# Sharing an activation-table stay between the Silu of z and the Silu of the next chunk's u

## The chip, the cores and the metric

The kernel runs on one core of a Trainium2 chip. The metric is the device time of one execution in microseconds (us), lower is better. A core has five engines that each work through their own instruction queue: TensorE (PE in the profile), VectorE (DVE), ScalarE (ACT), GpSimd (POOL) and SyncE (SP), which here only issues DMA transfers.

## The reference

The program is a stack of four residual layers on an image batch x of shape (8, 384, 32, 32), each `x = x + layer(groupnorm(x))`. Layers 0 and 2 are Mamba blocks, layer 2 with a layer norm before and an MLP behind; layers 1 and 3 are convolution blocks. The change touches only the Mamba blocks. Cut to what matters, one of them computes, for each image as a sequence of L = 1024 tokens:

```python
xz = x @ in_proj_w.T
xin, z = split(xz, 2)                  # 768 channels each
u = silu(causal_conv3(xin) + conv_b)
dt, Bm, Cm = split(u @ x_proj_w.T)     # 24, 16 and 16 columns
dt = softplus(dt @ dt_proj_w.T + dt_proj_b)
# for every channel d and state n (768 x 16):
h[t] = exp(dt[t] * A) * h[t-1] + dt[t] * u[t] * Bm[t]
y[t] = sum_n h[t] * Cm[t] + u[t] * D
y = y * silu(z)
return y @ out_proj_w.T
```

All inputs and outputs are fp32.

## The kernel before

**Tiling.** The work of a Mamba layer is cut into chunks of 512 tokens, two for each of 8 images and 16 for each of the two layers, so there are 32 chunks: 0 to 15 are layer 0, 16 to 31 are layer 2. The 768 channels are six blocks of 128, `NH` = 3 of them make a half. Each chunk has 24 steps (`NQ`); a step handles 32 channels times 16 states as four tiles of 128 x 512. The whole kernel is 768 steps in a fixed order, and everything else is threaded between them.

**One step.** A DMA broadcasts dt*u to a tile `g` of 128 x 2048 (`begins`, on SP, up to five such tiles). POOL multiplies `g` by B (`times`). PE spreads dt to the four PSUM tiles `dA` (`decays`), ACT turns each into exp(dt*A) in place (`exps`), DVE scans each tile (`scans`) and multiplies two of the four by C itself, POOL multiplies the other two by C (`states`), PE sums over the states into `y` (`gathers`). In the first chunk of an image ACT also copies the last column of each scan to `carry`, which the second chunk starts from. Every fourth step completes a channel block: DVE multiplies `y` by silu(z) (`gatings`), and this frees the single `y` bank for the next block.

**Table stays.** ACT holds one set of activation functions at a time. The steps need Exp and Ln; Silu and Gelu lie in other sets. So each visit to Silu or Gelu is a *stay*: a table load, the activations, and a load back, which `exp_set` (L369) issues at once. While it lasts the `exps` on ACT wait. There are four kinds: `gates(s, 0)` for the first half of z (z0 below), `gates(s, 1)` for the second half (z1), `front` for both halves of u, and the Gelus of layers 1 and 2. A stay starts only when `session` (L563) allows it: when at least `LEAD` = 2 exponentials are done that DVE has not scanned yet, or when it was held up for longer than `PATIENCE`.

**Who needs what.** z0 is used from the first gating of its chunk, z1 from the fourth, which follows step 15. The u of chunk n + 1 is projected while chunk n is in its steps 6 to 11, and its Silu must come early enough for x_proj, dt, softplus, three DMA stages (`dtd`, `dud` to DRAM and `dts`, `g` back) and POOL's first product before step 0 of chunk n + 1.

**Order.** Nothing is reordered on the chip: each engine's queue is written out in Python. `Order.run` (L219) holds generators such as `gates`, `front`, `finish`, `layer1`, and at each turn issues the next instruction of the one that the planner `Clocks` expects to begin first. Thus one instruction that begins at another planned time can shift which process comes next, on all engines. `once(test)` holds a process until a condition of the planner's state is true; `ahead["scans"]` counts scans issued, four for each step.

Of the kernel before, what the change touches and what calls it, by code (L numbers as in the profile page):

```python
# [11 lines left out]
AF = mybir.ActivationFunctionType  # L12
# [42 lines left out]
def _flat(ap):  # L55
    return ap.rearrange("p a b -> p (a b)")
# [193 lines left out]
def tile_conv_preact_d4(ctx: ExitStack, tc: tile.TileContext, a: dict, out: bass.AP):  # L250
# [23 lines left out]
    def new(pool, shape, dtype, tag, bufs=1, name=None):  # L274

        t = pool.tile(shape, dtype, tag=tag, name=name or tag, bufs=bufs)
        ring = rings.setdefault((id(pool), tag), [])
        if len(ring) >= bufs:
            clocks.born[t.name] = clocks.last.get(ring[-bufs], 0.0)
        ring.append(t.name)  # L280
        return t

    def on(engine, *aps, when=None, due=None, next_=False):


        def ready():
            t = when() if when else 0.0
            return None if t is None else max(t, clocks.known(*aps) if aps else 0.0)

        return engine, ready, due, next_  # L290
# [5 lines left out]
    def once(test):  # L296
        return None, lambda: 0.0 if test() else None, None, False

    class Tokens:
# [5 lines left out]
        def when(self):  # L305
            return min(self.free) if self.free else None
# [19 lines left out]
    def ps_give(ps, tag):  # L326
        banks.append((tag, clocks.last[ps.name]))
# [32 lines left out]
    def together(due, gens):  # L360

        made = [order.add(g, due) for g in gens]
        yield on(None, when=lambda: (
            None if any(p["done"] is None for p in made) else max(p["done"] for p in made)
        ))
# [3 lines left out]
    def exp_set():  # L369
        nc.scalar.preload_act_table_set(SET_EXP)  # L370
        clocks.free["ACT"] += 1.28
        act_set["now"] = "exp"

    def act(out_, in_, func, **kw):
        if func in (AF.Exp, AF.Ln):
            if act_set["now"] != "exp":
                exp_set()
        elif func not in (AF.Identity, AF.Copy, AF.Square, AF.Abs):
            if act_set["now"] != func:
                clocks.free["ACT"] += 1.28  # L380
            act_set["now"] = func
        scalar.activation(out_, in_, func, **kw)
# [175 lines left out]
    def projection(s, name, part, at):  # L558
        return chain(
            name, ((s["w"][part][:, k, at : at + P], s["xn"][:, k, :]) for k in range(KC))  # L560
        )

    def session():  # L563

        asked = []

        def ready():
            asked.append(order.now)
            late = order.now - asked[0] > PATIENCE
            late = late or ("begin", ahead["decays"] // 4) not in said  # L570
            return 0.0 if ahead["decays"] - ahead["scans"] >= LEAD or late or order.stuck else None

        return ready

    def gates(s, h):
        n = s["n"]
        yield once(lambda: "normed" in s and "loaded" in s["w"] and (n == 0 or chunks[n - 1]["gated"] >= (NH if h == 0 else ND)))
        z = s["z", h] = new(wk, [P, NH, T], F32, "z", 2)

        def block(d):  # L580
            ps, tag = yield from projection(s, "ps_z", "z", (h * NH + d) * P)
            yield on("ACT", ps)
            act(z[:, d, :], ps, AF.Copy)
            ps_give(ps, tag)

        yield from together(s["t"] + (6 if h else -4), [block(d) for d in range(NH)])
        yield on("ACT", z, when=session())
        act(_flat(z), _flat(z), AF.Silu)
        exp_set()
        s["gates", h] = True  # L590
# [30 lines left out]
    def front(s):  # L621
        c, n, due = s["c"], s["n"], s["t"] - 26
# [40 lines left out]
        if c > 0:  # L663
            yield on("POOL", *u, due=-1)
            prev = chunks[n - 1]["xt"]
            hal = new(wk, [P, ND, 3], F32, "hal")
            gpsimd.tensor_mul(
                hal[:, :, 0:2], prev, vec[:, :, 0:1].to_broadcast([P, ND, 2])
            )
            gpsimd.tensor_mul(hal[:, :, 2:3], prev[:, :, 1:2], vec[:, :, 1:2])  # L670
            gpsimd.tensor_add(hal[:, :, 0:1], hal[:, :, 0:1], hal[:, :, 2:3])
            for h in range(2):
                gpsimd.tensor_add(
                    uh[h][:, :, 0:2], uh[h][:, :, 0:2], hal[:, h * NH : (h + 1) * NH, 0:2]
                )
        yield on("ACT", *u, when=session())
        for h in range(2):
            act(_flat(uh[h]), _flat(uh[h]), AF.Silu)
        exp_set()
# [86 lines left out]
    ahead = {"decays": 0, "scans": 0}  # L766
# [499 lines left out]
    def layer3(s):  # L1266
# [68 lines left out]
    chunks = [  # L1335
        {"pre": pre, "src": src, "b": b, "c": c, "n": (q * B + b) * NCH + c, "gated": 0}
        for q, (pre, src) in enumerate((("l0_", a["x"]), ("l2_", x_mid)))
        for b in range(B)
        for c in range(NCH)
    ]  # L1340
# [4 lines left out]
    def start_jobs(t):  # L1345
        n, i = divmod(t, NQ)
        if i or n >= len(chunks):
            return
        s = chunks[n]
        order.add(gates(s, 1), t + 8)  # L1350
        if s["c"] == 0 and n + NCH < len(chunks):
            m = chunks[n + NCH]
            order.add(measured(m), t + NQ + 4)
        if n + 1 < len(chunks):
            later = chunks[n + 1]
            order.add(front(later), t + NQ - 26)
            order.add(gates(later, 0), t + NQ - 4)
        order.add(finish(s), t + NQ + 10)
# [15 lines left out]
    def begun():  # L1374
        yield once(lambda: "fronted" in chunks[0])
        order.add(gates(chunks[0], 0), 1)
        start_jobs(0)
# [3 lines left out]
    order.add(load_mamba("l0_"), 0)  # L1381
    order.add(load_mamba("l2_", chunks[B * NCH - 1]), NQ * B * NCH - 30)
    order.add(front(chunks[0]), 0)
    order.add(begun(), 0)
    order.add(diagonal(), 2)
# [151 lines left out]
```

## Time and profile before

| what | value |
|---|---|
| median of 3 runs | 6210.31 us (6209.75 to 6211.98) |
| the profiled execution: its own time, its span | 6204.07 us, 6202.2 us |
| DVE busy | 5616.8 us, 91% |
| POOL busy | 5725.3 us, 92% |
| PE busy | 5799.2 us, 94% |
| ACT busy | 4241.3 us, 68% |
| table loads | 288, of 1283 ns each, 369.6 us in all |
| Silu of half a z | 64, of 1485 ns each |
| Silu of half a u | 64, of 1477 ns each, two in each stay |

Busy is the time in which an engine executes something; the rest of the span is idle. 6202.2 us over 768 steps is 8.1 us for each step, start and end included; from the first step's scans to the last step's, the mean is 7.82 us. An instruction is named by the tile that it writes, an arrow, and the tiles that it reads: `dA<-dA,w_A` is one exponential. Nearly all instructions carry line 189, the line of a wrapper, so they are told apart by tiles and shapes; L370 is the load back of a stay.

### The profile page before, as it was taken

Reading aid. Unit: us, or ns where it says so; the run is one execution under the profiler, and the core shown is the slowest. Engines: PE = TensorE matmul, PEld = TensorE weight load, DVE = VectorE, ACT = ScalarE, POOL = GpSimd, SP = SyncE. Lnnn points to the kernel's source line nnn. Section 1 sums busy time; section 2 is a strip of 40 time slices with the busy share of each in tenths; the row PEclk is TensorE's granted clock in tenths of the full one; section 3 lists DMA queues with packets and bytes.
Section 4 is the critical chain, followed back from the end, with each engine's and each line's share of the span. In section 5 each row is a group of like instructions: output and inputs, shape, how many; then the busy total and the mean of one; then the engine's idle time right before and its main releaser. Section 6 shows DMA issues by size and latency. Waiting matters only on the chain.

```text
span 6202.2 us, 62614 instructions
## 1 busy us (share of the span) xinstructions
PE 5799.2 (94%) x19022; PEld 2184.1 (35%) x19022; DVE 5616.8 (91%) x6381; ACT 4241.3 (68%) x7942; POOL 5725.3 (92%) x2028
## 2 busy tenths in 40 slices
PE   6878999999999999999989999999999999999998
PEld 2223333333333333333333333333333333333333
DVE  5999999999998999998887899899998999989994
ACT  5656677677667767776676676777767777677753
POOL 4999999999999999989997999999999999999991
PEclk8889999999999999999999999999999999999999
DMA  6877878877887888787777888878888788888871
GB/s 178 193 184 186 195 190 194 204 188 193 190 193 185 196 205 189 192 205 186 180 185 183 199 196 219 200 198 209 198 215 201 200 207 198 212 205 197 207 197 58
DMA packets 346724, 1195.88 MB, mean 193 GB/s; under 512 B 40516, under 2 KB 142580, under 8 KB 248084
## 3 DMA queue, kind: packets, MB, share of 16 engines
q1 hardware_dynamic: 346388, 1191.88, 79.1%
q8 instruction: 152, 2.49, 0.2%
q14 instruction: 184, 1.51, 0.1%
HBM read 1040.73 MB, written 150.99 MB: 192 GB/s over the span
## 4 chain that ended last, share of the span: by engine, by line
DVE 25%; PE 13%; POOL 8%; DMA 4%; issue 4%; ACT 4%; SPq 0%; POOLq 0%; DVEq 0%; ACTq 0%
DVE g L189 11%; DVE dA L189 8%; POOL g L189 6%; DVE u L189 2%; PE ps_dn L189 2%; PE ps_up L189 2%; PE ps_dw L189 2%; PE y L189 2%; PE dA L189 2%; DMA g<-dud 2%; DVE ps_dw L189 1%; PE ps_z L189 1%; DMA dts<-dtd 1%; PE ps_out L189 1%; DVE st L189 1%
## 5 line engine op out<-in xcount | busy, mean ns | idle before, releaser
L189 POOL TENSOR_TENSOR g<-g,bc 128x1024 f32<-128x1024 f32 (+1 forms) x1536 | 5243.4, 3447 | 248.1 <-ACT carry L189 94.1
L189 ACT ACTIVATE dA<-dA,w_A 128x512 f32<-128x512 f32 x3072 | 2018.6, 661 | 931.0 <-PE dA L189 919.4
L189 PE MATMUL dA<-dts,selr 96*128 96x512 bf16 x3072 | 1190.0, 390 | 233.2 <-DVE g L189 207.6
L189 DVE TENSOR_TENSOR_SCAN g<-dA,carry,g 128x512 f32<-128x512 f32 x768 | 955.4, 1269 | 75.1 <-POOL g L189 61.1
L189 DVE TENSOR_TENSOR g<-dA,bc 128x512 f32<-128x512 f32 x1536 | 994.5, 677 | 17.3 <-ACT carry L189 16.4
L189 DVE TENSOR_TENSOR_SCAN g<-dA,g 128x512 f32<-128x512 f32 x768 | 909.4, 1209 | 85.7 <-POOL g L189 77.8
L189 DVE TENSOR_TENSOR_SCAN dA<-dA,carry,g 128x512 f32<-128x512 f32 x768 | 952.2, 1271 | 28.0 <-ACT dA L189 27.4
L189 DVE TENSOR_TENSOR_SCAN dA<-dA,g 128x512 f32<-128x512 f32 x768 | 909.0, 1212 | 62.3 <-ACT dA L189 61.7
L189 PE MATMUL y<-g,sely 128*32 128x512 f32 x6144 | 857.0, 627 | 38.0 <-POOL g L189 35.6
L189 PEld LDWEIGHTS <-selr 96*128 96x128 bf16 x3072 | 300.2, 98 | 1113.0 <-issue 1072.0
L189 PE MATMUL ps_in<-xf,w_in 128*128 128x512 f32 x1152 | 562.7, 610 | 10.0 <-ACT xf L189 7.6
L189 PE MATMUL ps_z<-xf,w_z 128*128 128x512 f32 x1152 | 567.8, 597 | 3.6 <-DVE dt L189 3.6
L189 PE MATMUL ps_up<-t,mw 128*128 128x512 f32 x1152 | 556.0, 596 | 7.1 <-DVE u L189 5.2
L189 PE MATMUL ps_out<-u,w_out 128*128 128x512 f32 x1152 | 547.5, 594 | 0.4 <-ACT carry L189 0.4
L189 PE MATMUL ps_dn<-h,mw 128*128 128x512 f32 x1152 | 545.3, 594 | 1.6 <-ACT h L189 1.6
L189 PE MATMUL ps_dw<-tp,diag 128*128 128x512 f32 x864 | 438.8, 609 | 9.6 <-ACT diag L189 9.6
L189 PEld LDWEIGHTS y<-g,sely 128*32 128x32 f32 x6144 | 126.3, 109 | 599.2 <-issue 313.0
L189 PEld LDWEIGHTS ps_in<-xf,w_in 128*128 128x128 f32 x1152 | 218.6, 195 | 263.8 <-issue 234.2
L189 POOL TENSOR_TENSOR dt<-dt,u 128x512 f32<-128x512 f32 x192 | 244.3, 1274 | 72.4 <-PE ps_dr L189 56.3
L189 PEld LDWEIGHTS ps_dn<-h,mw 128*128 128x128 f32 x1152 | 217.8, 190 | 259.9 <-issue 235.3
L189 PEld LDWEIGHTS ps_up<-t,mw 128*128 128x128 f32 x1152 | 214.4, 190 | 267.2 <-issue 230.4
L189 PEld LDWEIGHTS ps_z<-xf,w_z 128*128 128x128 f32 x1152 | 215.9, 191 | 252.7 <-issue 215.2
(118 smaller groups left out, 6451.1 us busy)
## 6 DMA issues: line engine op xcount, KB each, us to landing
g<-dud SPq DMA_DIRECT2D x768, 1024.0 KB, 8.2
dtd<-pc SPq DMA_DIRECT2D x192, 384.0 KB, 4.0
dts<-dtd SPq DMA_DIRECT2D x192, 384.0 KB, 7.8
mw<-in_l_mlp_w SPq DMA_DIRECT2D x192, 384.0 KB, 6.5
dud<-dt SPq DMA_DIRECT2D x768, 64.0 KB, 3.2
xf<-in_x SPq DMA_DIRECT2D x16, 768.0 KB, 9.1
x<-in_x SPq DMA_DIRECT2D x16, 768.0 KB, 11.9
x_mid<-x SPq DMA_DIRECT2D x16, 768.0 KB, 7.0
```

The costliest lines, as they stand in the source:

```text
L189: return call(out_, *args, **kw)
```

## The change

`gates(s, 1)` no longer goes into a stay of its own once z1 is projected. It leaves its tile in `s["gate"]` and waits. The `front` of the next chunk now waits until the previous chunk's `gate` entry exists, enters its stay, and there computes the Silu of that z1 ahead of the two of u. If `front` has not done so by the time 13 steps of the chunk are scanned in the planner's state, `gates` takes its tile back and goes into a stay of its own as before. The last chunk has no next one and stays as it was.

```diff
         yield from together(s["t"] + (6 if h else -4), [block(d) for d in range(NH)])
+        if h == 1 and n + 1 < len(chunks):
+            s["gate"] = z
+            yield once(lambda: ("gates", 1) in s or ahead["scans"] >= 4 * (s["t"] + 13))
+            if ("gates", 1) in s:
+                return
+            s["gate"] = None
         yield on("ACT", z, when=session())
         act(_flat(z), _flat(z), AF.Silu)
         exp_set()
...
+        prev = chunks[n - 1] if n > 0 else {"gate": None}
+        yield once(lambda: "gate" in prev)
         yield on("ACT", *u, when=session())
+        if prev["gate"] is not None:
+            act(_flat(prev["gate"]), _flat(prev["gate"]), AF.Silu)
+            prev["gates", 1] = True
         for h in range(2):
             act(_flat(uh[h]), _flat(uh[h]), AF.Silu)
         exp_set()
```

## The prediction

> **What bounds the kernel now.** I read the page's totals first, then the groups of instructions with shapes kept apart, then the waits, then windows over single stays.
>
> ```profile
> PE 5799.2 (94%) x19022; PEld 2184.1 (35%) x19022; DVE 5616.8 (91%) x6381; ACT 4241.3 (68%) x7942; POOL 5725.3 (92%) x2028
> ```
>
> POOL and DVE are both nearly full, PE looks so, and ACT, the engine that the change relieves, has a third of its time free.
>
> ```profile
> L189 POOL TENSOR_TENSOR g<-g,bc 128x2048 f32<-128x2048 f32 x768 | 3479.6, 4535 | 90.5 <-DMA g<-dud 76.5 <-PE dA L189 3.3 <-PE ps_dn L189 3.1
> L189 ACT ACTIVATE dA<-dA,w_A 128x512 f32<-128x512 f32 x3072 | 2018.6, 661 | 931.0 <-PE dA L189 919.4
> ...
> L189 ACT ACT_TABLE_LOAD x144 | 184.8, 1283 | 3.3 <-PEq L1527 0.7
> L370 ACT ACT_TABLE_LOAD x144 | 184.8, 1283 | 2.5
> ...
> L189 ACT ACTIVATE z<-z 128x1536 f32<-128x1536 f32 x64 | 95.0, 1485 | 0.7
> L189 ACT ACTIVATE u<-u 128x1536 f32<-128x1536 f32 x64 | 91.5, 1477 | 0.4
> ```
>
> Behind the bar stand busy time and mean ns of one, then idle time before them. POOL alone needs 4.54 + 2.36 us a step (its 128x1024 row is 2359 ns) of the mean 7.82. A z stay is 1.28 + 1.49 + 1.28 = 4.05 us of ACT, a u stay 5.5. ACT idles 919 us waiting for PE's `dA`, so it hurts only when DVE or POOL run dry. The waits say how often:
>
> ```profile
> DVE g L189 <- POOL g L189: 139.0, 77, 7.8
> ...
> POOL g L189 <- ACT carry L189: 94.1, 54, 7.1
> ...
> DVE dA L189 <- ACT dA L189: 89.2, 64, 3.5
> ```
>
> (Total us, times, longest.) DVE waits 89 us for exponentials, POOL 94 us for carries from ACT, and DVE 139 us for POOL. Windows over single stays, each to 4 us past its end (us, then busy times):
>
> ```profile
> 4588.20:4596.30 8.10, 7.98 (x26) 2.84 (x25) 8.10 (x11) 8.04 (x15) 8.10 (x4) 1.00 0.93 236
> 4710.60:4718.70 8.10, 8.04 (x28) 3.16 (x27) 3.75 (x5) 7.98 (x12) 8.10 (x5) 1.00 1.03 194
> ```
>
> The first is the z1 stay of chunk 24: DVE (third pair) is busy 8.10 of 8.10, so the stay costs it nothing. The second is a z0 stay: DVE idles 4.35, but the timeline puts that wait on POOL's `g`, not on ACT. Over all 31 z1 stays with a successor such windows give 23.1 us of DVE idle, 12.6 in the 16 that will matter below, and at most 0.03 each in chunks 19 to 29. **So a z1 stay as it stands is nearly free.**
>
> **What the Trainium skill says.** "ScalarE: Activation LUTs", What ACT_TABLE_LOAD costs: about 1283 ns for the load plus 1380 ns of DRAIN. The trace agrees on the load and shows no drain: the three parts of the stay at 4588.25 follow within 0.02 us. The same page, Table sets, advises batching by set, which is the change. "Perfetto Trace Analysis", Identifying the Most-Contended Engine: occupancy is a fair measure for Vector, Scalar and GPSIMD, matmul busy is not; so I take POOL and DVE as the bound and not PE's 94%. "PSUM — Partial Sum Buffer", Engine vs sequencer instructions: Scalar, Vector and GpSimd queues are strict FIFO. The trace agrees (in every stay the exponentials stand behind the loads), so where a stay is put decides what waits.
>
> **What the change really does to the order.** The order written for the changed kernel has 256 table loads, not 288: 128 stays, 16 fewer and not 31. Only the z1 of chunks 0-3, 6, 7, 10-16, 19, 23 and 29 shares its stay. In the other 15 the time-out at 13 scanned steps wins: z1's own stay moves from about steps 2-8 to step 13.5, and u's, which stood at 12.5 to 14, follows 0.25 to 4 steps later (8.5 in chunk 17, whose u waits for the change of layer). So:
>
> 1. Removed: 16 x 2 x 1.283 = 41 us of ACT. Worth, off ACT's queue: the 12.6 us of DVE idle above, plus some POOL idle (2.2 to 3.0 us behind the z1 stays of chunks 6, 10, 12, 14 while it waits for a carry). I take -18; bounds -24 and -10.
> 2. Lengthened: the 16 shared stays by one Silu, 1.49 us. DVE's idle at u stays averages 1.7 us, so the two scans it has in hand are used up in part of them. All exposed is 16 x 1.49 = 24, all hidden 0; I take half, +12.
> 3. Moved: 15 z1 stays to just ahead of u's. The 10.5 us of idle there go. The nearest row for a stay shortly after another is the z0 stay of chunk 25, three steps after u's: 1.84 us of DVE idle. Ten of them at that price: +18. In chunks 4, 8, 21, 25 and 27 z0 follows too, three stays within two steps: 4.08 + 5.45 + 4.08 = 13.6 us, 8 exponentials 5.3, and ACT's other work (4241 busy - 2019 exponentials - some 727 in stays) / 768 = 1.95 a step, 3.9: 22.8 us in 15.6. ACT falls 7 behind; against one 1.84 paid before I take +5 each, +25. Together 18 + 25 - 10.5 = +32; bounds -10 (the cover seen at z1 in layer 2 holds here) and +60.
> 4. Delayed: u, and what it issues: x_proj, per channel block a softplus chain, one `dtd` DMA (4.0 us to landing), four `dud` (3.2), `dts` (7.8) and four `g` (8.2), all in SP's one queue, where later `g` stand behind a late `dud`. In chunk 18, where everything waits for it, the trace shows 51.9 us from the end of u's stay to the first scan, at no load; elsewhere about 80 pass and 28 are slack. In the new order chunk 29's u stay stands 6.5 steps ahead of its first scan, 6.5 x 7.8 - 5.5 = 45 us: a stall of 6 to 7. Chunks 27 and 31 (7.75 and 8.5 steps) just make it. +6; bounds 0 and +60.
> 5. Reshuffled on all engines. One thing can be priced: by how many steps POOL's `times` runs ahead of its `states`. In the trace, DVE's idle before a step's first scan is 1.51 us in the mean at lead 0, 0.19 at lead 1, 0.03 at lead 2. Without the start-up chunk, lead 0 goes from 39 to 32 steps, lead 1 falls by 38: -10.6 - 7.2 = -17. Pairs of chunks with the same work differ by up to 7 us in the trace (layer 0: 354.6 to 361.9), so 16 reshuffled pairs may sum to 10 or 15 either way.
> 6. At nothing: the gatings with z1. In the new order the fourth still follows step 15, and z1 is ready two steps earlier; if it weren't, `y`'s one bank would stop PE at 1 step's price, 8 us. The last part of layer 2's w_z load waits for z1 of chunk 15, six steps later now; its first use moves by one step, hidden behind the steps.
>
> Sum: -18 + 12 + 32 + 6 - 17 = +15, and +3 at the end (six more `ps_dn` matmuls behind the last step, by 545.3 / 1152 = 0.47 us each): **+18**. The profiled execution (6204.07, its span 6202.2) goes to 6222; the median stands 6.2 above it, so 6228.
>
> **Rivals.**
> - *Bunched stays and a late u cost more than the loads save* (my forecast): 6228. For it: point 3's arithmetic, and z1's present stays being free. Against: ACT has 32% to spare. Chance 0.32; own range 6215 to 6250.
> - *Starvation at chunk starts*: the softplus chains of chunks 25 to 31 miss the prefetch, a small copy of chunk 18's start (41.3 us for one step). At 15 us in four chunks: 6285, with point 3 less; I say 6265. Chance 0.14.
> - *Wash*: the moved stays are covered as before, 5 us net: 6212. Chance 0.26. (0.2%, or 12.4 us, is about what a measurement of this kernel can tell from no change.)
> - *Faster*: exponentials and carries come earlier everywhere. Points 1 and 5 at full, -24 and -17, 2 at nothing, 3 at its lower bound -10: -51, or half of that with reshuffling: about 6180. It decides this way if DVE's two-scan cover is intact when the joint stay starts, so DVE's idle at it stays at u's 1.7 us. For it: POOL's lead grows. Against: POOL and DVE keep all their work. Chance 0.28.
> - *The change does all it says* (31 shared): the built order excludes it.
>
> So slower 0.46, within 0.2% 0.26, faster 0.28; all but the tails of both rivals lie between 6168 and 6278.
>
> **What would show it.** 256 loads; z1 in shared stays with DVE idle up to 3 us; in chunks 4, 8, 21, 25 and 27 a rise of DVE's wait for `dA` by 3 to 6 us each; a POOL wait on `g<-dud` at the start of chunk 29. DVE's total wait for ACT `dA` should rise above 89 us while POOL's for carries stays near 94. I am wrong if these fall together, or if the time leaves the range: then the order, not the stays, decided.

## The result, and the profile after

The changed kernel takes 6249.15 us in the median (6248.03 to 6254.24), the one before 6210.03: a ratio of 1.0064 with a 95% interval of 1.0049 to 1.0079. It is **slower by 39 us**. The profiled execution has a span of 6246.2 us, against 6202.2.

The totals of the page after, in the columns of the first fence of the prediction:

```profile
PE 5800.3 (93%) x19022; PEld 2190.3 (35%) x19022; DVE 5615.7 (90%) x6381; ACT 4197.7 (67%) x7910; POOL 5722.7 (92%) x2028
```

DVE, POOL and PE do the same work to a few microseconds; ACT does 43.6 us less. So nothing was added: the 44 us of span are idle time. The groups of the changed kernel with shapes kept apart:

```profile
L189 ACT ACTIVATE dA<-dA,w_A 128x512 f32<-128x512 f32 x3072 | 2016.1, 661 | 950.2 <-PE dA L189 936.9 <-ACT sq L189 0.3
L189 POOL TENSOR_TENSOR g<-g,bc 128x1024 f32<-128x1024 f32 x768 | 1810.2, 2358 | 206.5 <-ACT carry L189 143.8 <-DVE g L189 61.3 <-PE ps_dt L189 1.0
...
L189 ACT ACT_TABLE_LOAD x128 | 164.2, 1283 | 2.9 <-PEq L1538 0.7
L370 ACT ACT_TABLE_LOAD x128 | 164.2, 1283 | 2.2
```

There are 256 table loads, 128 stays: 16 fewer, as the built order said, and not 31. The waits of DVE (total us, times, longest), same kernel:

```profile
DVE dA L189 <- ACT dA L189: 148.5, 85, 4.1
DVE g L189 <- POOL g L189: 110.8, 66, 5.7
...
DVE g L189 <- ACT dA L189: 31.1, 20, 3.5
```

Before, DVE waited 89.2 + 11.9 us for exponentials (scans that write `dA` and scans that write `g`), now 148.5 + 31.1: 78 us more, though ACT has less to do. (11.9 is the row `DVE g <- ACT dA` of the kernel before.) Its wait for POOL's `g` fell by 28, from 139.0. POOL's wait for carries from ACT rose from 94.1 to 143.8. DVE's four largest waits for PE (`ps_dn`, `y`, `ps_dw`, `ps_out`) fell together from 192.7 to 142.3 us, so PE with its 93% is not what held it up more. The engine that was relieved is now waited for longer. Why?

### The profile page after: what moved, and what is told of

Same layout as the page of the kernel before. It is cut to its first block, busy times and chain, and to the rows that moved or that the text cites. A ratio compares the mean times of both kernels' runs of the same rounds, so it can differ in the third digit from the quotient of the medians.

```text
span 6246.2 us, 62641 instructions
## 1 busy us (share of the span) xinstructions
PE 5800.3 (93%) x19022; PEld 2190.3 (35%) x19022; DVE 5615.7 (90%) x6381; ACT 4197.7 (67%) x7910; POOL 5722.7 (92%) x2028
## 4 chain that ended last, share of the span: by engine, by line
DVE 24%; PE 16%; POOL 10%; ACT 7%; issue 6%; DMA 3%; SPq 0%; DVEq 0%; POOLq 0%; ACTq 0%
DVE g L189 11%; POOL g L189 8%; DVE dA L189 8%; DMA g<-dud 3%; PE ps_dw L189 3%; PE ps_up L189 3%; PE y L189 2%; PE ps_dn L189 2%; PE dA L189 2%; ACT dA L189 2%; DVE u L189 2%; PE ps_in L189 1%; DVE ps_dw L189 1%; PE ps_out L189 1%; ACT L370 1%
## 5 line engine op out<-in xcount | busy, mean ns | idle before, releaser
L189 POOL TENSOR_TENSOR g<-g,bc 128x1024 f32<-128x1024 f32 (+1 forms) x1536 | 5240.6, 3445 | 288.5 <-ACT carry L189 143.8
```

What stands on the lines that cost most here:

```text
L189: return call(out_, *args, **kw)
```

## Two twins without z1's Silu

Two theories stood against each other. *Stays*: z1's Silu is now in worse places, next to u's or lengthening it. *Order*: the queues of all engines were interleaved anew, and that costs whatever z1's Silu does. To tell them apart, both kernels were built with their plans unchanged, so that every other instruction keeps its place on every engine, and z1's Silu simply not issued (the remarks behind # are added here):

```diff
-        act(_flat(z), _flat(z), AF.Silu)
-        exp_set()
+        if h == 1 and n + 1 < len(chunks):
+            planned_silu(_flat(z))     # the planner's clock moves, nothing is issued
+            clocks.free["ACT"] += 1.28
+            act_set["now"] = "exp"
+        else:
+            act(_flat(z), _flat(z), AF.Silu)
+            exp_set()
```

**In the order before** (label e1_before_no_z1).

> The kernel before with every instruction in its place on every engine, but without the Silu of z1 and its two table loads in chunks 0 to 30 (31 stays; the output lacks that Silu). It prices all z1 stays at their old places. Theory 'stays' (the changed kernel is slower because its stays expose DVE more: z1 bunched ahead of u, joint stays longer): the old places are nearly free, DVE idles 23 us in them, so 10 to 30 us faster than before, 6180 to 6200. Theory 'order' (the new interleaving of all engines costs, whatever the stays do): says the same here; what decides is the difference to the twin of the changed kernel.

Measured: 6199.45 us against 6206.29 of the kernel before on the same chip, ratio 0.9989 (0.9982 to 0.9995): 7 us faster (3 to 11), less than the 10 to 30 expected. DVE idled 23.1 us in those stays, so most of that idle was not lost time.

**In the changed order** (label e2_after_no_z1), where the joint stays keep u's two Silus alone. There `planned_silu` also stands in place of z1's Silu in `front`.

> The changed kernel with every instruction in its place, but without the Silu of z1 in chunks 0 to 30 and without the loads of its 15 own stays (the output lacks that Silu). Against the twin of the kernel before it compares the two orders with no z1 stay in either. Theory 'stays': the two twins are within 10 us of each other and this one is 45 to 65 us faster than the changed kernel. Theory 'order': this one is 25 to 40 us slower than its twin, some 6215 to 6230, and only 10 to 30 us faster than the changed kernel.

Measured: 6238.38 us, ratio 1.0052 (1.0039 to 1.0064). The twins have the same instructions, 226 table loads each, and differ only in order: by 6238.4 - 6199.5 = **39 us, the whole loss**. The time is above the 6215 to 6230 that 'order' named, and 'stays' is out. z1's Silu costs 7 us in the old order and about 7 in the new one: the changed kernel stands 39 us above the kernel before and its twin 32. These two were measured at different times, and their intervals leave the second 7 open from nothing to some 19; the 39 between the twins is known to about 9. DVE's waits of the two twins, the old order first:

```profile
DVE g L189 <- POOL g L189: 138.0, 76, 7.8
DVE dA L189 <- ACT dA L189: 87.4, 63, 3.5
```

```profile
DVE dA L189 <- ACT dA L189: 146.5, 85, 4.1
DVE g L189 <- POOL g L189: 115.2, 74, 5.8
```

They repeat the shift of before and after, with z1's Silu in neither. 'Stays' as I had meant it falls. What remains of it concerns every *other* stay: DVE's waits for ACT ahead of a scan, as far as they lie inside those stays, are 49 us in the first twin and 95 in the second. The u stays of layer 2 show it best. In the kernel before DVE does 2.8 us of work other than scans during each, in the mean, and up to 2 us past its end it idles 0.6 us. In the changed kernel the 11 that hold u alone meet 1.05 us of such work, and DVE idles 2.3. The work of DVE beside the scans (below: side work) that used to lie under the stay lies elsewhere now.

## The price of a longer stay, and the change as it was meant

**One more pass in each u stay, order unchanged** (label e3_before_long_u):

```diff
             act(_flat(uh[h]), _flat(uh[h]), AF.Silu)
+            if h == 0 and n > 0:
+                nc.scalar.activation(_flat(uh[0]), _flat(uh[0]), AF.Identity)   # not told to the planner
```

> The kernel before in its order, with one more pass of 128x1536 (Identity, in place, about 1.48 us) inside each u stay of chunks 1 to 31: the lengthening that sharing a stay brings, alone and 31 times. All exposed it is +46 us, hidden 0. Forecast by the prediction's half: +23 us. Theory 'stays' +23 to +46; theory 'order' 0 to +15.

Measured: 6237.46 us, ratio 1.0049 (1.0037 to 1.0062): +31 us (23 to 38) for 31 passes of 1.48 us, 1.0 us each, more than my half and inside the range named for 'stays': at the old places a longer u stay does cost. The trace says where: in layer 2 each pass that lies in the first chunk of an image costs 1.5 us from chunk 24 on, and those in the second chunks cost nothing (chunks 21, 23 and 27: 0.0). Windows over two u stays of the kernel before, in chunk 24 and in chunk 25, each to 2 us past its end, show the difference:

```profile
4644.90:4652.40 7.50, 7.08 (x22) 2.63 (x23) 6.38 (x7) 7.46 (x11) 7.34 (x6) 1.00 0.78 167
4832.90:4840.40 7.50, 7.18 (x24) 2.67 (x25) 7.47 (x11) 7.24 (x7) 7.50 (x2) 1.00 0.74 193
```

In the first DVE (third pair) already idles 1.12 us, with 1.35 us of side work during the stay; in the second it idles 0.03, with 4.4 us of side work. Where it had run dry, a longer stay is all loss.

**Sharing without any reshuffling** (label e9_share_old_order). The first twin, with z1's Silu issued at the head of the next u stay, at u's old place. PE, DVE, POOL and SP keep the order before, instruction by instruction.

```diff
+        z = chunks[n - 1].get("gate") if n > 0 else None
+        if z is not None:
+            nc.scalar.activation(_flat(z), _flat(z), AF.Silu)                    # not told to the planner
         for h in range(2):
             act(_flat(uh[h]), _flat(uh[h]), AF.Silu)
```

> The change as it is meant, with no reshuffling: on PE, DVE, POOL and SP the order is that of the kernel before, instruction by instruction; on ACT the Silu of z1 stands at the head of the next chunk's u stay in 30 chunks, and its own stay is gone (228 table loads; chunk 17 keeps its own because its next u comes too late). Theory 'order' (the loads save what the z1 stays cost, 7 us by the first twin; a longer u stay costs 1.0 us each by the third run; all else is order): -7 + 30 = +23, 6222 to 6238 if before is 6206 to 6210. If z1's own stays had hidden costs that leaving them out did not show, or joint stays are cheaper than a pass of Identity at the same place, it is at or below before. If z1 comes too late for its gating, over +40, with DVE waiting in u<-y,z.

Measured: 6231.07 us against 6204.39, ratio 1.0042 (1.0028 to 1.0056): +27 us. So the two prices add up, -7 + 30 to within the noise, and they answer the design question: **even with 30 stays really merged and the other engines' order unmoved, the change loses**. The groups of this kernel show that it did merge them:

```profile
L370 ACT ACT_TABLE_LOAD x114 | 146.3, 1283 | 2.0
L189 ACT ACT_TABLE_LOAD x84 | 107.8, 1283 | 2.2 <-PEq L1542 0.7
...
L691 ACT ACTIVATE z<-z 128x1536 f32<-128x1536 f32 x30 | 44.5, 1484 | 0.3
L691 ACT ACT_TABLE_LOAD x30 | 38.5, 1283 | 0.4
```

114 + 84 + 30 = 228 loads. 60 loads of 1.283 us, 77 us of ACT, are saved at stays that cost the kernel next to nothing (the first twin), and 30 x 1.48 = 44 us are added in stays where two thirds of a longer pass are paid for (the run before).

## More sharing, less sharing

**A later time-out** (label e4_timeout16): `ahead["scans"] >= 4 * (s["t"] + 16)`.

> The changed kernel with the time-out at 16 scanned steps instead of 13: 29 z1 share u's stay and two keep their own (230 table loads), at the price of z1 coming as late as it can. Theory 'stays' (the 15 bunched stays are the loss): most of the loss gone, 6205 to 6225. Theory 'order' (any new interleaving costs): 6225 to 6260. If z1 is too late for the fourth gating, slower still, with DVE or PE waiting at step 16.

Measured: 6277.54 us, ratio 1.0119 (1.0103 to 1.0135), +71, above the ranges of both theories. Nearly twice the merges, nearly twice the loss, but not in the same places. With each chunk counted from the last scan of the one before to its own, layer 0 merges 16 stays instead of 12 and stands only about 4 us above the kernel before, where the changed kernel stands 16; layer 2 stands 68 above. Chunk 31 alone takes 230.3 us instead of 199.1; its u stay stood at step 18.5 in this order, which brings up the next theory.

**Layer 0 only** (label e5_layer0_only): `if h == 1 and n + 1 < B * NCH`, and `front` of layer 2 doesn't wait.

> Sharing (and the wait of z1) in chunks 0 to 14 alone; from chunk 17 on the order is that of the kernel before (266 loads, u stays of layer 2 back at steps 12.8 to 14). Theory 'late u' (the loss sits where u's stay slips and the next chunk starts without prefetch): layer 2's 22 us and the end's 5 go, what stays is layer 0's 16 us, of which chunk 10 with no lead at its start holds 8: +12 to +20 over before, 6218 to 6230. Theory 'any new order costs about the same everywhere': half of the loss stays, also near +20, but spread evenly over chunks 3 to 15. If sharing itself were good, below 6210.

Measured: 6222.59 us against 6206.46, ratio 1.0024 (1.0013 to 1.0034), +16. Chunk by chunk the trace repeats the changed kernel in layer 0 (chunk 10 +7.8 us, 11 +4.9, 14 -5.8) and the kernel before in layer 2 (within 1.0 from chunk 18 on). So the loss has two parts that stand by themselves: 16 us in layer 0, 22 in layer 2, with 5 at the end. Single traces tell layer 0 only roughly: in the run with a late u below, its order there is that of the kernel before, and its trace still stands 9 us above.

**Holding without sharing** (label e7_hold_no_share): time-out at 8 steps, so z1 is held and then always goes alone.

> The changed kernel with the time-out at 8 scanned steps: z1 is held until then and always goes alone (288 loads, nothing is shared). The order shows u's stays of layer 2 slipping all the same: 15.5, 16.2, 15.2, 16.2, 15.2 and 17.5 ahead of chunks 21, 23, 25, 27, 29 and 31. Theory 'late u': slower although no stay is shared or longer, +20 to +40, with chunk 31 losing 12 to 20 and 23 and 27 5 to 10 each. Theory 'sharing costs': within 10 of before.

Measured: 6298.12 us, ratio 1.0148 (1.0132 to 1.0163): **+92 us with not one stay shared or lengthened**, far beyond what either theory expected. Chunks 23, 27 and 31 lose 15.5, 14.8 and 10.3 us, about as the late u would have it, but chunks 4 and 12 in layer 0, which I had not named, lose 27.6 and 19.4. The wait of z1 alone sets off a new order, and that is enough for a loss.

## Is it the late u?

In layer 2 the u projections wait for a tile of u that the output projection two chunks earlier frees; that waits for the MLP of the chunk before it, and the MLP for its two Gelu stays. In the built order, the first Gelu stay slips from mostly steps 17.8 to 18.5 to steps 19.5 to 22.5, and u's stay ahead of chunk 29 from step 13.5 to 17.5. Windows over that chunk's first three steps, before and after (us, then busy times of PE, PEld, DVE, ACT, POOL):

```profile
5498.70:5524.20 25.50, 24.69 (x79) 9.17 (x78) 20.64 (x23) 19.55 (x27) 23.90 (x10) 1.00 0.85 193
```

```profile
5520.40:5559.20 38.80, 38.80 (x114) 15.89 (x113) 25.55 (x27) 24.70 (x42) 33.10 (x14) 1.00 0.96 254
```

38.8 us instead of 25.5, with 13 us of DVE idle instead of 5, and with 5 us more work of DVE, 9 of POOL and 35 more matmuls in these steps. The timelines of the changed kernel show what DVE and POOL did at the turn of the chunk:

```profile
5527.56 0.69 DVE L189 SCALAR_TENSOR_TENSOR dt<-ps_dt,spm 128x512 f32<-128x512 f32 x1 [2.53 <-ACT spm L189]
5530.09 0.75 DVE L189 SCALAR_TENSOR_TENSOR x<-ps_dn,vec,x 128x512 f32<-128x512 f32 x1 [1.85 <-PE ps_dn L189]
5530.81 2.46 DVE L189 TENSOR_TENSOR_SCAN g<-dA,carry,g 128x512 f32<-128x512 f32 x2
```

```profile
5525.15 1.15 POOL L189 TENSOR_TENSOR pc<-spm,pc 128x512 bf16<-128x512 f32 x1
5526.26 4.52 POOL L189 TENSOR_TENSOR g<-g,bc 128x2048 f32<-128x2048 f32 x1
```

The last scan of chunk 28 ended at 5520.4. POOL's first product of chunk 29 starts only at 5526.26, behind softplus work of the next blocks, and DVE scans when it is done, at 5530.81. Before, that product began 2.3 us ahead of the last scan's end. Two runs test it.

**A late u by hand, with no sharing** (label e6_late_u_alone), in the kernel before. The planner knows of the delay, so from chunk 20 on the queues of DVE, ACT and POOL are in a new order here too:

```diff
+        late = {21: 15, 25: 16, 29: 17}.get(n)
+        if late:
+            yield once(lambda: ahead["scans"] >= 4 * (s["t"] - NQ + late))
         yield on("ACT", *u, when=session())
```

> The kernel before, nothing shared and z1 not held, but u's stay ahead of chunks 21, 25 and 29 held back by hand until 15, 16 and 17 steps are scanned. In the order written the stays then stand at steps 15.5, 19.5 and 17.5 (chunk 27 14.2, chunk 31 15.5). Theory 'late u': a dose shows. 51.9 us are needed from the end of the stay to the first scan, a step is 7.8: chunk 21 loses 0 to 3 us, chunk 29 10 to 18 as in the changed kernel, chunk 25 20 to 35; in all +30 to +55, 6240 to 6265. Theory 'order in general': these three chunks lose no more than their neighbours, total within 15 of before.

Measured: 6265.52 us, ratio 1.0095 (1.0080 to 1.0110), +59, just past the top of what 'late u' named. Chunk 21 (stay at step 15.5) loses 1.0 us, chunk 29 (17.5) 5.7, chunk 25 (19.5) 25.9 and the chunk ahead of it 12.5. So the chunks with a late u lose, and steeply more the later it is; the new order behind it can have a part in that. But at the same step 17.5 chunk 29 loses 15.4 in the changed kernel and 5.7 here, under the 10 to 18 expected: the position does not set the price by itself.

**u's stay no longer held back in the changed kernel** (label e8_u_not_held): `yield on("ACT", *u)` without `when=session()`. (`session` has one more way out than was told above: a stay may also start when the `g` of the step whose exponentials come next has not been issued.)

> The changed kernel, with the u stay no longer waiting for two exponentials in hand (260 loads, 14 shared). In the order, the stays ahead of chunks 27 and 29 come back from 16.2 and 17.5 to 15.0 and 14.5, and the steps with lead 0 fall from 32 to 25. Theory 'late u': chunks 27 and 29 get back most of their 8 and 15 us, so 15 to 25 us faster than the changed kernel: 6222 to 6235. Theory 'order in general': within 10 of 6249.

Measured: 6263.19 us, ratio 1.0091 (1.0076 to 1.0106): **slower still, the forecast missed**. Its part came true: chunks 27 and 29 stand 5.2 and 2.4 us above the kernel before, instead of 8.2 and 15.4. But the new order loses the 16 us elsewhere and more: chunk 25 goes from -1.7 to +10.4, chunk 13 from +0.2 to +7.6, chunk 14 from -5.8 to +3.8. And DVE idles 2.7 us at the u stays that stand alone in layer 2, in place of 2.3; that can come from starting without two exponentials in hand, but the order has changed as well.

So a late u goes with dear chunk starts, and moving the stay back returned 16 of the 24 us of chunks 27 and 29; other chunks of layer 2 gain in the changed kernel (18: -8.4, 24: -4.4). It is not *the* cause of the loss. **What stays open**: why each new order lost. Every one tried here did, by 16 to 92 us. All five (the runs e4 to e8) share with the changed kernel that DVE waits more for exponentials and POOL more for carries (119 to 148 us against 94.1). But the size of these waits doesn't follow the loss. With z1 held and nothing shared DVE waits 129.5 us for exponentials (101 before), at +92 us; the changed kernel waits 179.6, at +39. And the longer u stay in the old order raises POOL's wait for carries to 118 as well. I tried no order that was rebuilt with the planner's costs corrected, and cannot say whether new orders lose as a rule or only these.

## Why the prediction was right or wrong

The direction (slower, 0.46) and the range held, the own range by 1 us; the size, +18, was less than half of +39. That the direction came out right was luck. The terms for the stays, 1 to 3, were to bring +26; the twins put z1's stays at 7 us in either order, so they brought about nothing. The terms for the order, 4 and 5 with the 3 us at the end, were to bring -8, and brought the whole +39.

1. *Removed loads, -18*: too much. All 31 z1 stays together cost 7 us (first twin). "Nearly free" was right; but not even the 12.6 us of DVE's idle came back, let alone POOL's on top.
2. *Longer stays, +12*: too little as idle, and too much as time. In windows to 4 us past the 16 joint stays DVE idles 51.3 us, in the same windows of the twin without z1's Silu 31.0: 20 us more, 1.3 for each stay. Yet all of z1's Silu costs the changed kernel only about 7 us, so most of this idle seems to be made up for elsewhere. (At the old places a pass of that length did cost 1.0 us of time.)
3. *Bunched stays, +32*: **the step that failed.** All of z1's Silu costs about 7 us in the new order, joint and bunched stays together. I had charged 25 us for ACT falling behind in chunks 4, 8, 21, 25 and 27, where three stays stand within two steps. The sign I had named for it came: DVE's wait for `dA` there rose by 8.1, 4.5, 7.2, 2.6 and 0.6 us. But it has another cause, since the twin without z1's Silu shows the same. Chunk 21, before, after, and that twin:

```profile
DVE dA L189 <- ACT dA L189: 2.0, 2, 1.8
```

```profile
DVE dA L189 <- ACT dA L189: 9.2, 3, 3.8
```

```profile
DVE dA L189 <- ACT dA L189: 8.4, 3, 3.3
```

The times of these five chunks in the changed kernel and in its twin lie within 1.4 us of each other.

4. *Late u, +6*: the place, chunk 29, was right, the size too small: 15.4 there and 8.2 in chunk 27, which I had let "just make it". From the end of u's stay to the first scan of chunk 29 pass 57.7 us. The 51.9 us of chunk 18, the time at no load, run to the end of that scan; to its start they are 50.6. The wait was not the one I had named: in the window over the chunk's start POOL never waits for `g<-dud`, it is busy with the softplus work of other blocks.
5. *Reshuffling, -17*: right as far as it went and misleading. DVE's wait for POOL fell by 28. But I priced only the wait that the new order shortens. The other side, DVE's and POOL's waits for ACT, which rose by 78 and 50, has no such sign in the order of one engine, and I left it at "10 or 15 either way". The twins put the order at +39.
6. *Nothing for the gatings*: right; DVE's wait for `y` in `u<-y,z` fell, from 57.3 to 34.0.

Of the signs named, POOL's wait for carries was to stay near 94 us and rose to 143.8, which spoke against my account from the first. Of the rivals, *starvation* was half seen (chunks 27 and 29). *Faster* is out in this order. It was to be decided by DVE's idle at the joint stay staying at u's 1.7 us, and that is 3.2 in the mean; and removing every z1 stay from the kernel before gains only 7 us. I had named this outcome as one that "the order, not the stays, decided", but expected to see it as a time outside the range.

No version here beats the kernel before. With some 7 us to win from z1's stays in the old order and 1.0 us in the mean to pay for each lengthening, a mixture (sharing only in the second chunks of an image, say, where the longer pass cost nothing) can win about 0.1% there, and none was tried.

## What to carry to other kernels

Before merging two visits to an activation table, ask what the waiting engine has in hand at each of them: a stay that lies under other work is nearly free, and moving its Silu to one that doesn't can cost more than the two table loads save. Where the order of the queues is generated, a change of one process moves them all: hold the order fixed and leave out or add the one operation, and the price of the operation and the price of the order come apart, in two runs (the twins here). A wait that gets shorter in a new order says little until the waits that get longer have been counted. And a sign that was forecast can come for another reason: look for it in the twin too.

## What was not expected of the hardware

ScalarE's own time says little of what a stay costs: 31 stays, 31 x 4.05 = 126 us of ScalarE with its table loads, cost 7 us of the kernel's time. The price depends on the place, and sharply: the same 1.48 us pass costs 1.5 us in the first chunks of layer 2's images, where VectorE has 1.35 us of side work during the stay, and 0.0 in the second ones, where it has 4.4.
